# Chunk sums turned back one scan slot later, two copies and the softmax factors at higher priority, factors spread a step later

## The chip, the cores and the metric

The kernel runs on one core of one Trainium2 chip. A core has five engines that run side by side, each through its own queue in order: PE (TensorE, matmuls and transposes, writing to PSUM banks), DVE (VectorE), ACT (ScalarE), POOL (GpSimd) and SP (SyncE, which here issues transfers between main memory and the on-chip buffer). The metric is the time of one execution in microseconds on the device. Three runs of the kernel before gave 5039.27, 5041.66 and 5051.98 us; the median is 5041.66 us.

## What is computed

Two layers on a batch of 8 images of 384 channels and 32x32 positions, that is 1024 tokens, all in 32-bit floats. Layer 0 is a selective scan in both directions over the tokens, plus a gated 3x3 convolution. Layer 1 is causal attention with 6 heads of 64, then a feed-forward part with sign weights and quantised activations (for the first five images alone). Cut to what the change touches:

```python
# layer 0, for u forward and backward; h has 16 states per channel
def step(h, inp):
    dA, dBu, c = inp                      # exp(delta*A), delta*u*B, C
    h = dA * h + dBu
    return h, einsum('bdn,bn->bd', h, c)  # the sum over the 16 states
y = ys + u * D_param
y = y * silu(z)
out = einsum('bld,od->blo', y, out_proj_w)

# layer 1
scores = where(causal, einsum('bhqd,bhkd->bhqk', q, k), -inf)
attn = softmax(scores)
out = einsum('bhqk,bhkd->bhqd', attn, v)
```

## The kernel before

**The scan stream.** For each image (order 0, 1, 2, 3, 5, 6, 4, 7) there are four parts (direction and half of the tokens), 16 states and three chunks of 128 channels. A unit is one chunk, one part and two states: 96 units an image, 768 in all. A unit passes through four stages:

- `s_first` (L585): POOL multiplies delta*u by the row of B into a buffer `g` of 128x1024 (L588). There are six such buffers.
- `s_scan` (L591): for each of the two states ACT makes the decay (L601) into one of two PSUM banks, DVE runs the recurrence in place in `g` (L606), POOL copies the carry (L611) and multiplies `g` by the row of C (L612).
- `s_sum` (L614): PE adds the states up. Eight transposing matmuls against the identity (L620) turn the unit's two 128x512 halves into the one PSUM bank `y`, adding over 4 or 8 successive units of the same chunk and half. With the last of these (`closes`) the bank is emptied into the on-chip buffer: by a copy on ACT (L635) for the first and the last of such a group's runs, by an addition on DVE (L639) for those between. Only then may the next chunk's sums enter the bank.
- `s_gate` (L641): after a chunk's last run, the two partial sums are turned back (L659) onto a matmul of u with diag(D) (L654), in a bank of the kind "pt"; DVE multiplies by the gate (L668), and the result goes to main memory, where the attention of that image reads it. There are 48 such gates.

`slots` (L1093) writes the order down: slot k issues `s_first` of unit k+2, `s_scan` of unit k, `s_sum` of unit k-1 and `s_gate` of unit k-1.

**The other stream.** Beside the slots run the work ahead of the scan for later images and, once an image's scan is through, its attention and feed-forward part. Each is a list of steps with a nominal length; `run` and the loop at the end of the kernel merge the steps with the slots by these lengths. The slots up to number 96 (`first`, L1121) go beside the preparation of the next images, the rest (`others`, L1122) beside attention and feed-forward.

**Attention.** `probabilities` makes, for each pair of heads c and each half g of the queries, the exponentials of the scores in blocks of up to 512 keys, each with its own maximum `nm` and sum `rs`. `weighted_values` (L820) then walks over the 4 or 8 chunks j of keys, one step for each:

- `factors` (L825) at j = 0: from `nm` and `rs` the factor of each block. For g = 0 one reciprocal, for g = 1 six small operations on DVE (L833, L834, L836 to L839) and an exponential on ACT (L835).
- `spread` (L841) at j % 4 = 2: eight small matmuls (L847) spread a block's factors over 64 rows each into a "pt" bank, ACT copies them out (L854).
- `turned` (L856): PE transposes the probabilities (L862) into "pt" banks, ACT copies them (L864).
- `weigh` (L867), one step behind: PE multiplies by the values (L875) into the one bank "av". After a block's fourth chunk DVE multiplies this bank by the spread factors (L889, L891).

PSUM has eight banks: one "y", two "da", two "s", two "pt", one "av".

**What sets the order.** A scheduler puts the instructions into the engines' queues when the kernel is built. It takes, among the instructions that it holds to be ready, the one of the highest priority; priority is the order in which the kernel's text issues them, and `tc.high_priority(offset=60)` counts an instruction as if it had been issued 60 earlier. Waits between engines are put in by the same program. On the chip each queue then runs as it was written.

Of the kernel before, what the change touches and what calls it, by code (L numbers as in the profile page):

```python
# [12 lines left out]
ALU = mybir.AluOpType  # L13
# [23 lines left out]
QT = HB // P  # L37
# [7 lines left out]
AHEAD = 2  # L45
# [9 lines left out]
def kernel(  # L55
# [16 lines left out]
    nc = tc.nc  # L72
# [17 lines left out]
    def mtile(name, n=L):  # L90
        return mid.tile([P, n], F32, name=name, tag="mid")
# [7 lines left out]
    def bank(name, tag=None):  # L99
        if tag is None:  # L100
            turn[0] += 1
            tag = ("s", "pt")[turn[0] % 2]
        return ps.tile([P, HB], F32, name=name, tag=tag, bufs=BANKS[tag])

    def half(h):
        return slice(h * HB, (h + 1) * HB)

    def chunk(c):
        return slice(c * P, (c + 1) * P)
# [434 lines left out]
    class Unit:  # L544
# [6 lines left out]
    units = [  # L551
        Unit(b, part, c, n)
        for b in ORDER
        for part in range(len(PARTS))
        for k in range(NS // SET)
        for c in (range(NC) if k % 2 == 0 else reversed(range(NC)))
        for n in range(k * SET, (k + 1) * SET, 2)
    ]
# [17 lines left out]
    def s_row(u, i):  # L576

        if not u.asks:
            return
        r = sp.tile([P, 2, HB], F32, name=f"bc{i}_{u.name}", tag=f"bc{i}", bufs=4)  # L580
        rows = spilled[u.b, "rows", u.d][i * NS + u.n : i * NS + u.n + 2, half(u.h)]
        load(r, rows.partition_broadcast(P))
        sst["bc", i, u.b, u.part, u.n] = r
# [30 lines left out]
    def s_sum(u):  # L614
        if u.opens:
            sst["y"] = bank(f"y_{u.name}", "y").rearrange("p (j k) -> p j k", k=P)
        y, g = sst["y"], sst.pop(("g", u.name))
        for i in range(2):
            for j in range(QT):
                nc.tensor.matmul(  # L620
                    out=y[:, j, :],
                    lhsT=g[:, i, chunk(j)],
                    rhs=ident,
                    is_transpose=True,
                    start=(u.opens and i == 0 and j == 0),
                    stop=(u.closes and i == 1),
                    skip_group_check=True,
                )
        if not u.closes:
            return  # L630
        key = ("yt", u.b, u.c, u.h)
        if u.run == 0 or u.last:
            tag = {"tag": "yl", "bufs": 1} if u.last else {"tag": "yt", "bufs": 2 * NC}
            yt = sp.tile([P, QT, P], F32, name=f"yt_{u.name}", **tag)
            nc.scalar.copy(yt, y)  # L635
            sst[key] = sst.get(key, []) + [yt]
        else:
            (yt,) = sst[key]
            nc.vector.tensor_tensor(yt, yt, y, ALU.add)  # L639

    def s_gate(u):  # L641

# [31 lines left out]
    def attention(b, emit_ffn, emit):  # L674
# [83 lines left out]
        def at_once(second):  # L758
            return tc.high_priority(offset=HURRY) if second else nullcontext()

        def rows_of(e):
            return slice(e * HD, (e + 1) * HD)
# [57 lines left out]
        def weighted_values(c, g, steps):  # L820


            last = (g + 1) * QT - 1

            def factors():  # L825

                nm, rs = st["nm", c, g], st["rs", c, g]
                st["f", c, g] = mtile(f"f_{b}_{c}_{g}").rearrange("p (k l) -> p k l", k=2)
                if g == 0:
                    nc.vector.reciprocal(rs, rs)  # L830
                    return
                low = small.tile([P, QT, 2, 1], F32, name=f"low_{b}_{c}", tag="low")
                nc.vector.tensor_reduce(low, nm, AX.X, ALU.min)  # L833
                nc.vector.tensor_tensor(nm, low.to_broadcast([P, QT, 2, 2]), nm, ALU.subtract)  # L834
                nc.scalar.activation(nm, nm, AF.Exp)  # L835
                nc.vector.tensor_tensor(rs, rs, nm, ALU.mult)  # L836
                nc.vector.tensor_reduce(low, rs, AX.X, ALU.add)
                nc.vector.reciprocal(low, low)
                nc.vector.tensor_tensor(rs, nm, low.to_broadcast([P, QT, 2, 2]), ALU.mult)  # L839

            def spread(kb):  # L841

                fp = bank(f"f_{b}_{c}_{g}_{kb}", "pt")
                for i in range(QT):
                    for e in range(2):
                        f = st["rs", c, g][:, i, e, kb : kb + 1]
                        nc.tensor.matmul(  # L847
                            out=fp[rows_of(e), chunk(i)],
                            lhsT=f.to_broadcast([P, HD]),
                            rhs=ident,  # L850
                            start=True,
                            stop=True,
                        )
                nc.scalar.copy(st["f", c, g][:, kb, :], fp)  # L854

            def turned(j):  # L856
                cols = slice(max(j - g * QT, 0) * P, HB)
                for e in range(2):
                    pt = bank(f"pt_{b}_{c}_{g}_{j}_{e}", "pt")
                    for i in range(max(j - g * QT, 0), QT):  # L860
                        pr = st["pr", c, g, i, j // QT]
                        nc.tensor.transpose(pt[:, chunk(i)], pr[:, e, chunk(j % QT)], ident)  # L862
                    ptn = ptp.tile([P, HB], F32, name=f"ptn_{b}_{c}_{g}_{j}_{e}", tag=f"ptn{e}")
                    nc.scalar.copy(ptn[:, cols], pt[:, cols])  # L864
                    st["ptn", j, e] = ptn

            def weigh(j):  # L867
                if j % QT == 0:
                    st["av"] = bank(f"av_{b}_{c}_{g}_{j}", "av")
                av = st["av"]  # L870
                cols = slice(max(j - g * QT, 0) * P, HB)
                for e in (1, 0):
                    hd = 2 * c + e
                    with at_once(e == 0):
                        mm = nc.tensor.matmul(  # L875
                            out=av[rows_of(e), cols],
                            lhsT=st["v"][:, j, hd * HD : (hd + 1) * HD],
                            rhs=st["ptn", j, e][:, cols],
                            start=(j % QT == 0),
                            stop=(j % QT == QT - 1),  # L880
                        )
                    if e == 0:
                        pin(mm)
                if j % QT < QT - 1:
                    return
                kb = j // QT
                o, f = st["o"][:, c, half(g)], st["f", c, g][:, kb, :]
                if kb == 0:
                    nc.vector.tensor_tensor(o, av, f, ALU.mult)  # L889
                else:  # L890
                    nc.vector.tensor_tensor(av, av, f, ALU.mult)  # L891
                    nc.vector.tensor_tensor(o, o, av, ALU.add)

            for j in range(last + 1):

                @steps
                def _(j=j):
                    if j == 0:
                        factors()
                    if j % QT == 2:  # L900
                        spread(j // QT)
                    turned(j)
                    if j > 0:
                        weigh(j - 1)

            @steps
            def _():
                weigh(last)
# [184 lines left out]
    def slots(lo, hi):  # L1093
        def at(f, k):
            if 0 <= k < len(units):
                f(units[k])

        def slot(k):
            at(s_load, k + AHEAD + 2)
            at(lambda u: s_row(u, 0), k + AHEAD + 2)  # L1100
            at(lambda u: s_row(u, 1), k + 2)
            at(s_first, k + AHEAD)
            at(s_scan, k)
            at(s_sum, k - 1)
            at(s_gate, k - 1)

        return [(lambda k=k: slot(k), 5.0) for k in range(lo, hi)]

# [9 lines left out]


    per, ahead = len(units) // B, 3  # L1120
    first = slots(-AHEAD - 2, per + 1)  # L1121
    others = slots(per + 1, len(units) + 1)  # L1122

    taps = btile("taps").rearrange("p c l -> p (c l)")[:, : NC * DCONV * P]
    taps = taps.rearrange("p (c k q) -> p c k q", c=NC, k=DCONV)
# [37 lines left out]
    at = 0.0  # L1163
# [57 lines left out]
```

## Time and profile before

| | |
|---|---|
| median of three runs | 5041.66 us |
| the profiled execution's own time | 5052.48 us |
| its span | 5050.7 us |
| instructions | 50731 |
| mean granted TensorE clock | 0.883 |
| L620 sums on PE | 6144, 920.6 us busy |
| L635 copies of the bank on ACT | 96, 580 ns each |
| L639 additions of the bank on DVE | 56, 674 ns each |
| L847 spread of factors on PE | 1152 records, 100.0 us busy |
| L854 copies of spread factors on ACT | 72, 576 ns each |
| L601 decays on ACT | 1536, 691 ns each |
| L606 recurrences on DVE | 1536, 1210 or 1271 ns each |

In the profile's groups the columns are line, engine, operation, result <- operands, shapes and count; then busy time in us and the mean of one in ns; then the idle time of the engine just before these instructions and what ended it. PEld is the loading of weights, which overlaps the matmuls. A line of the wait view names the engine and the line that waited, what it waited for, the total in us, the number of waits and the longest. In the timeline the columns are start and length in us, engine, line, operation; in square brackets the idle time of the engine before it and what ended it.

### The profile page before, as it was taken

How to read it: one execution, taken by the hardware profiler on the slowest of the kernel's cores; microseconds unless marked ns; L12 is line 12 of the kernel's file. 1: busy time of each engine (PE TensorE's matmuls, PEld its weight loads, DVE VectorE, ACT ScalarE, POOL GpSimd, SP SyncE). 2: the span in 40 equal slices, each digit the busy share in tenths (PEclk: the TensorE clock that was granted, in tenths of full speed). 3: DMA queues.
4: the chain of work that ended last, by engine and by line, in shares of the span. 5: the costliest groups of instructions: out<-in, count | busy, mean ns of one | idle time of the engine just before them, and what ended most of it. 6: DMA issues, size and time to landing. Idle time of an engine off the chain costs nothing. (4 is left out here: it accounts for less than half of the span.)

```text
span 5050.7 us, 50731 instructions
## 1 busy us (share of the span) xinstructions
PE 4072.5 (81%) x16458; PEld 2180.7 (43%) x16458; DVE 3605.3 (71%) x4775; ACT 2667.4 (53%) x4850; POOL 3689.9 (73%) x1944
## 2 busy tenths in 40 slices
PE   4687787888888888788788888887787978978899
PEld 1243343444444444344444444443454444444444
DVE  6887988676887767786778867688766666676623
ACT  4565664564554655545656446555465355464426
POOL 0578687896868976778876688867788988888700
PEclk7788797989889889888999889998898989989999
DMA  6554546323453334463334633334533334334210
GB/s 227 204 175 160 200 155 229 109 88 118 152 187 135 119 115 154 139 200 111 103 134 143 213 111 128 110 123 155 194 132 106 118 108 143 109 101 139 88 58 26
DMA packets 365009, 696.35 MB, mean 138 GB/s; under 512 B 30104, under 2 KB 88904, under 8 KB 364744
## 3 DMA queue, kind: packets, MB, share of 16 engines
q1 hardware_dynamic: 355232, 676.97, 40.0%
q10 hardware_dynamic: 9512, 16.15, 0.9%
q8 instruction: 130, 2.13, 0.2%
q14 instruction: 135, 1.11, 0.1%
HBM read 527.33 MB, written 165.68 MB: 137 GB/s over the span
## 5 line engine op out<-in xcount | busy, mean ns | idle before, releaser
L588 POOL TENSOR_TENSOR g<-ud,bc 128x1024 f32<-128x1024 f32 x768 | 1837.9, 2393 | 654.0 <-PE y L620 523.0
L612 POOL TENSOR_TENSOR g<-g,bc 128x1024 f32<-128x1024 f32 x768 | 1819.4, 2369 | 194.9 <-DVE g L606 132.4
L601 ACT ACTIVATE da<-dl,amat 128x512 f32<-128x512 f32 x1536 | 1055.9, 691 | 1515.1 <-DVE g L606 1489.8
L606 DVE TENSOR_TENSOR_SCAN g<-da,g 128x512 f32<-128x512 f32 x768 | 907.7, 1210 | 509.6 <-POOL g L588 496.3
L606 DVE TENSOR_TENSOR_SCAN g<-da,carry,g 128x512 f32<-128x512 f32 x768 | 955.1, 1271 | 403.9 <-POOL g L588 374.5
L620 PE MATMUL y<-ident,g 128*128 128x128 f32 x6144 | 920.6, 297 | 210.3 <-POOL g L612 122.3
L620 PEld LDWEIGHTS y<-ident,g 128*128 128x128 f32 x6144 | 766.9, 153 | 644.3 <-issue 345.5
L786 PE MATMUL s<-k,q 64*128 64x512 f32 (+3 forms) x1152 | 394.6, 602 | 134.6 <-DVE nm L800 113.5
L800 DVE CUSTOM_DVE_ANT_0 pr<-s,cmask 128x512 f32<-128x512 f32 (+3 forms) x576 | 298.9, 544 | 179.3 <-PE s L786 159.9
L810 ACT ACTIVATE pr<-pr,nm 128x512 f32<-128x512 f32 (+3 forms) x576 | 348.4, 606 | 125.1 <-DVE nm L800 123.5
L862 PE MATMUL pt<-ident,pr 128*128 128x128 f32 x1728 | 302.1, 304 | 83.5 <-ACT ptn L864 38.5
L992 PE MATMUL hp<-t,w 128*128 128x512 f32 x720 | 339.3, 618 | 25.4 <-DMA w<-w1s 21.2
L1036 PE MATMUL yp<-h,w 128*128 128x512 f32 x720 | 331.9, 620 | 32.0 <-DMA w<-w2s 27.6
L341 PE MATMUL in<-xn,win 128*128 128x512 f32 x576 | 291.2, 651 | 36.5 <-DVE xc L463 15.9
L862 PEld LDWEIGHTS pt<-ident,pr 128*128 128x128 f32 x1728 | 207.0, 152 | 243.5 <-ACT ptn L864 94.3
L875 PE MATMUL av<-ptn,v 128*64 128x512 f32 (+3 forms) x1152 | 274.3, 559 | 23.2 <-DVE o L889 17.2
L611 POOL COPY carry<-g 128x2 f32<-128x2 f32 x384 | 87.7, 228 | 271.2 <-DVE g L606 271.2
L864 ACT COPY ptn<-pt 128x512 f32<-128x512 f32 (+3 forms) x576 | 254.7, 473 | 55.5 <-PE pt L862 53.5
L725 PE MATMUL qp<-t,wqk 128*128 128x512 f32 x576 | 267.8, 616 | 14.7 <-DVE t L302 12.5
L400 DVE SCALAR_TENSOR_TENSOR loc<-xn,vec,loc 128x496 f32<-128x496 f32 (+3 forms) x384 | 259.5, 722 | 20.3 <-ACT loc L389 19.0
L786 PEld LDWEIGHTS s<-k,q 64*128 64x128 f32 x1152 | 134.8, 206 | 266.5 <-DVE nm L800 190.1
L1036 PEld LDWEIGHTS yp<-h,w 128*128 128x128 f32 x720 | 141.9, 201 | 204.7 <-issue 177.2
(153 smaller groups left out, 4753.4 us busy)
## 6 DMA issues: line engine op xcount, KB each, us to landing
bc<-rows SPq DMA_DIRECT2D x512, 512.0 KB, 4.1
dl<-sdl SPq DMA_DIRECT2D x160, 256.0 KB, 2.9
ud<-sud SPq DMA_DIRECT2D x160, 256.0 KB, 2.7
t<-st SPq DMA_DIRECT2D x63, 512.0 KB, 5.1
su<-u SPq DMA_DIRECT2D x48, 512.0 KB, 3.6
du<-su SPq DMA_DIRECT2D x96, 256.0 KB, 3.8
sdl<-du SPq DMA_DIRECT2D x96, 256.0 KB, 2.9
sud<-du SPq DMA_DIRECT2D x96, 256.0 KB, 2.7
```

What stands on the lines that cost most here:

```text
L341: nc.tensor.matmul(out=mp, lhsT=st["win", c][:, k, i, :], rhs=st["xn"][:, k, half(h)], start=(k == 0), stop=(k == NC - 1),)
L588: pin(nc.gpsimd.tensor_tensor(g, ud, sst["bc", 0, u.b, u.part, u.n], ALU.mult))
L601: nc.scalar.activation(da, sst["dl", u.b, u.c, u.part], AF.Exp, scale=amat[:, u.c, n : n + 1])
L606: nc.vector.tensor_tensor_scan(gi[:, ::step], da[:, ::step], gi[:, ::step], first, ALU.mult, ALU.add)
L612: pin(nc.gpsimd.tensor_tensor(g, g, sst["bc", 1, u.b, u.part, u.n], ALU.mult))
L620: nc.tensor.matmul(out=y[:, j, :], lhsT=g[:, i, chunk(j)], rhs=ident, is_transpose=True, start=(u.opens and i == 0 and j == 0), stop=(u.cl ...
L786: mm = nc.tensor.matmul(out=ss[e][:, : k1 - k0], lhsT=st["q"][rows_of(e), c, chunk(qi)], rhs=st["k"][rows_of(e), c, k0:k1], start=True, st ...
L800: nc.vector.tensor_tensor_reduce(out=x, in0=ss[e][:, :w], in1=mask, scale=-1.0, scalar=-MASKED, op0=ALU.add, op1=ALU.min, accum_out=m,)
L810: nc.scalar.activation(x, x, AF.Exp, bias=m, scale=-1.0, accum_out=rs[:, i, e, kb : kb + 1])
L862: nc.tensor.transpose(pt[:, chunk(i)], pr[:, e, chunk(j % QT)], ident)
L992: nc.tensor.matmul(out=hp, lhsT=st["w1"][:, c, chunk(m % 2)], rhs=st["xn"][:, c, half(h)], start=(c == 0), stop=(c == NC - 1),)
L1036: nc.tensor.matmul(out=yp, lhsT=st["w2", k // 6][:, k % 6, :], rhs=st["h", k // NC][:, k % NC, half(h)], start=(k == 0), stop=(k == NF - 1),)
```

## The change

Four edits, none of which changes what is computed:

- `s_gate` of a unit is issued one slot later, after the sums of the following unit; the slots' range is one longer, and the border between `first` and `others` moves by one.
- The two instructions that empty the bank `y` (L635 and L639) are issued at a priority 60 places higher.
- So are all instructions of `factors`.
- `spread` is issued in the step j % 4 = 3 instead of 2, that is one step after, and in the same step as the block's last `turned`; `weigh` of that last chunk, with the products L889 or L891 that read the factors, follows in the next step as before.

```diff
@@ s_sum
-            nc.scalar.copy(yt, y)
+            with tc.high_priority(offset=60):
+                nc.scalar.copy(yt, y)
             sst[key] = sst.get(key, []) + [yt]
         else:
             (yt,) = sst[key]
-            nc.vector.tensor_tensor(yt, yt, y, ALU.add)
+            with tc.high_priority(offset=60):
+                nc.vector.tensor_tensor(yt, yt, y, ALU.add)
@@ weighted_values
                     if j == 0:
-                        factors()
-                    if j % QT == 2:
+                        with tc.high_priority(offset=60):
+                            factors()
+                    if j % QT == QT - 1:
                         spread(j // QT)
                     turned(j)
                     if j > 0:
@@ slots
             at(s_sum, k - 1)
-            at(s_gate, k - 1)
+            at(s_gate, k - 2)
@@
-    first = slots(-AHEAD - 2, per + 1)
-    others = slots(per + 1, len(units) + 1)
+    first = slots(-AHEAD - 2, per + 2)
+    others = slots(per + 2, len(units) + 2)
```

## The prediction

> **What bounds the kernel now.** I read the page first (shares, then the costliest groups), then the waits, then three lines of code by their instructions, then the timeline around single stalls.
>
> ```profile
> PE 4072.5 (81%) x16458; PEld 2180.7 (43%) x16458; DVE 3605.3 (71%) x4775; ACT 2667.4 (53%) x4850; POOL 3689.9 (73%) x1944
> ...
> L588 POOL TENSOR_TENSOR g<-ud,bc 128x1024 f32<-128x1024 f32 x768 | 1837.9, 2393 | 654.0 <-PE y L620 523.0
> L612 POOL TENSOR_TENSOR g<-g,bc 128x1024 f32<-128x1024 f32 x768 | 1819.4, 2369 | 194.9 <-DVE g L606 132.4
> ```
>
> No engine is full. POOL does nothing but the scan: 768 units of two products, 2.39 + 2.37 us each, 3657 us in all, from 129 to 4812 us. So the scan stage lasts as long as POOL's work plus its idle time, and the largest piece of that idle time is 523 us in 203 waits for PE's sums (L620): a product of unit k+6 needs one of six buffers `g`, and PE frees it by turning unit k. PE works through one queue in order, so whatever stalls it there delays the sums behind it. The chain of waits holds only the last 450 us (from 4599 us) and says nothing of the stage itself.
>
> Which PE stalls the diff touches, from the wait view:
>
> ```profile
> PE yb L659 <- ACT yt L635: 58.7, 22, 9.8
> PE f L847 <- DVE rs L839: 57.3, 15, 8.5
> ...
> PE y L620 <- DVE yt L639: 44.0, 16, 7.2
> ...
> PE pt L862 <- ACT f L854: 34.3, 26, 3.9
> ```
>
> Each has total us, times, longest. The instructions of L847 add a second reason for the same place, a queue entry of ACT behind the factors, and those of L620 the other half of the bank waits:
>
> ```profile
>   DVE rs L839: 57.3, 15
>   ACT da L601: 16.2, 3
> ```
>
> ```profile
>   DVE yt L639: 44.0, 16
>   ACT yt L635: 29.4, 10
> ```
>
> So 73.5 us of PE stand still before the spread of the factors, 58.7 us before the turn-back of a chunk, 73.4 us before the next chunk's sums. Do these reach POOL? One stall in PE's timeline, and POOL's first product after it:
>
> ```profile
> 4080.99 1.08 PE L875 MATMUL av<-ptn,v 128*64 128x512 f32 x4
> 4087.83 1.98 PE L847 MATMUL f<-ident,rs 128*64 128x128 f32 x16 [5.75 <-DVE rs L839]
> ...
> 4093.08 1.04 PE L620 MATMUL y<-ident,g 128*128 128x128 f32 x8
> ```
>
> ```profile
> 4094.20 2.36 POOL L588 TENSOR_TENSOR g<-ud,bc 128x1024 f32<-128x1024 f32 x1 [6.55 <-PE y L620]
> ```
>
> PE waits 5.75 us for the factors; the sum behind them comes at 4093.08, and POOL has then been idle 6.55 us. I looked at all 17 stalls of over 1 us before L847: each is followed within 3 to 9 us by such a POOL wait, together 88 us. For the 22 turn-back stalls I took for each the smaller of the stall and POOL's waits for PE from 2 us before to 12 us after it: 42 of 58.7 us reach POOL. For the bank waits before L620 the same count gives only 18 of 73.4 us.
>
> **What the Trainium skill says.** "SBUF — State Buffer", Who interferes with whom: a VectorE instruction with two SBUF inputs and a GpSimd one that reads SBUF exclude each other, the later one blocks fully. The trace agrees: the factor steps L834, L836, L839 on 16 columns take 0.15 to 0.18 us at their shortest, but 1.3, 1.4 and 0.8 us in the mean and once 8.92 us, while POOL multiplies. So factors are late for a reason that no priority removes; only a later reader does. "TensorE: Matmul & The Clock Gate", Architectural detail: PE's queue only pulls weight loads ahead, ScalarE and VectorE are strictly first in, first out. The trace agrees: while PE stood from 4082 to 4087.8 us no other matmul ran. "ScalarE: Activation LUTs", What ACT_TABLE_LOAD costs: about 1283 ns a load; the trace shows 1283.
>
> **The change part by part.** Durations are of the profiled execution: span 5050.7 us, 5052.5 us with what lies around it; the median of the runs, 5041.66, is 10.8 lower. What a step is moved past I counted in the two built programs' queues, which hold no times.
>
> *Spread a step later.* The 1152 matmul records of L847 and the 72 copies L854 stay. Against the scan's units all attention work moves by about 0.9 unit, the f matmuls by 1.75, so they come 0.85 unit later than before among their neighbours. A unit lasts (4812 - 129)/768 = 6.1 us, so 5.2 us more cover; I use 5. Taking 5 from each of the 18 stalls leaves 7 us (3.5 of it from the 8.5 us one). Gone: 66 us. Nearly all of it reached POOL, but PE then runs on into readers of the same late DVE and ACT queues; that share is not to be read from the trace, between none and all of it. I take 70% kept: -47 us (bounds -66 and 0).
>
> Its price: the reader of the factors, L889/L891 on DVE, now starts a median 9.2 us after the copy L854 ends, at least 2.2 us. With the copy 5 to 6 us later, 6 to 10 of 72 readers would wait, 10 to 18 us of DVE with scans behind them: +5 us (bounds 0 and 18). In blocks on the diagonal the f bank is followed by one turn instead of two before its bank is wanted again (L862 <- f, 34.3 us today): +5 (0 to 10).
>
> *Gate a slot later.* Same instructions: 48 diagonal matmuls, 384 turns, 48 products L668, their loads and stores on SP, all one slot on. Before, the first to wait for the copied chunk is mostly the turn-back; after, always the next chunk's first sum, because the bank `y` is single. So this wait is moved, not removed. In 47 such places the PE work queued ahead of the first waiter has a median of 1.7 us before and 3.4 after, at 0.14 us for a turn and 1.12 for a 512-wide matmul; in the trace the 1.7 take 1.13 us, so 3.4 take 2.3, 1.2 us more cover. Taking 1.2 from each of the 22 stalls leaves 35: 24 us gone, 42/58.7 of it reaching POOL: -17 us (bounds -42 and 0). SP prefetches `us` and `z` when their single buffers come free; a slot's delay of both load and use cancels. The run of slots is one longer and all other work starts one slot later against the scan: in the tail the transpose of L960, which opens the last feed-forward product, stands behind one more unit of sums, 4.7 us of POOL: +5 us (0 to 6).
>
> *Copies and factors at higher priority.* No duration changes. In ACT's queue the copies stand a mean 4.7 units behind the scan's newest decay before and 4.8 after, in DVE's 8.0 and 7.9; factors move with their neighbours (0.83 unit against 0.9). The delay of a copy (start a mean 2.3 us after the sums on ACT, 2.9 on DVE) comes from scans and decays ahead of it that wait for POOL. -3 us (bounds -20 and 0).
>
> *Side effects.* Everything is reordered a little: four more table loads on ACT, 4 x 1.283 us = 5.1 us, beside an engine that is 53% busy, +1; three or four copies go from DVE to ACT, nothing.
>
> Sum: -47 +5 +5 -17 +5 -3 +1 = -51 us, so 5001.5 in the profile's time, a ratio of 0.990; on the median, 4991 us.
>
> **The rivals.**
>
> *The stall only moves on* (19%). PE gets past the factors, but the next thing in its queue needs DVE or ACT, and those were late. For: in the 8.92 us case DVE itself was held, and PE stands 109 us before scores L786 for DVE. Against: in the example it was followed by transposes, weights and sums that were ready. Then perhaps 20 of the 66 us and 5 of the turn-backs' 17 stay gained; with the costs of 16 us (5 + 5 + 5 + 1) that is -9 us, 5033 us.
>
> *Everything lands* (14%). All 66 us, 42 us of turn-backs, and copies prompt enough to give the 18 us of bank waits: -126 + 16 = -110, 4932 us.
>
> *The factors' reader holds DVE* (17%; slower). Where L889 waits for L854 in DVE's strict queue, scans wait behind it, then POOL. Cover between spread and reader falls from 8.9 to 5.0 us of PE work by the same counting. It needs ACT to be late: the copy starts a mean 1.03 us after the f matmuls, at most 5.3. At 1.5 us for each of 72 readers this costs 108 us against gains of 56 (the sum without the reader's 5): +52, 5094 us. It decides from 56/72 = 0.8 us a reader. Against: today's slack is 5.3 us or more for nine readers in ten.
>
> **How the numbers follow.** The forecast has 50%, its own range 4955 to 5026. All over, 4945 leaves out the better part of the large gain, 5060 takes in the stall that moves on and the light form of the slower rival; the bounds of the parts, all added on one side, would be -128 and +39 us, 4914 and 5081 on the median. This kernel's measurement can tell 0.3%, 15 us, from no change: faster than 5026.5 is the forecast, the large gain and nearly half of the moving stall (72%), the rest of the latter is within (11%), the reader's wait is slower (17%).
>
> **What would show it.** Right: waits of L847 for L839 and L601 fall from 73.5 to about 10 us; those of L659 for L635 go to nothing, those of L620 for L635 and L639 rise from 73 to about 105 us; POOL's waits for L620 fall from 523 to about 460. The slower rival would show L889 or L891 waiting for L854, absent today. The forecast is wrong if POOL's idle for L620 falls and its idle for L606 (132 before L612, 271 before L611) rises by as much, or if L847's waits stay.

## The result, and the profile after

The changed kernel takes 4982.55 us (median of four runs, 4979.25 to 4992.14) against 5040.47 us of the kernel before in the same comparison: a ratio of 0.9884, 95% interval 0.9863 to 0.9905. The forecast was 4991 us. The span of its profiled execution is 4982.3 us against 5050.7, 68 us less.

The page of the changed kernel, the engines' shares and POOL's two groups. Lines of the code have moved by two or three from L637 on: what was L639 is L641, L659 is L661, L847 is L849, L864 is L866, and the copy L635 is L636.

```profile
PE 4058.8 (81%) x16458; PEld 2192.3 (44%) x16458; DVE 3607.8 (72%) x4771; ACT 2668.1 (54%) x4858; POOL 3696.0 (74%) x1944
...
L588 POOL TENSOR_TENSOR g<-ud,bc 128x1024 f32<-128x1024 f32 x768 | 1840.4, 2396 | 579.8 <-PE y L620 452.0
L612 POOL TENSOR_TENSOR g<-g,bc 128x1024 f32<-128x1024 f32 x768 | 1822.1, 2373 | 251.7 <-DVE g L606 157.8
```

Work is the same to within 14 us on every engine; only the waiting has changed. POOL's idle time for PE's sums fell from 523 to 452 us; its idle time for the scans before L612 rose from 132 to 158, that before the carries L611 fell from 271 to 206. Over all of POOL's instructions, 71 us of waiting for PE and 47 us for DVE went, 12 us of other gaps went, and 48 us of waiting for transfers came: 1090 us of idle time before, 1008 after.

Three more lines of the wait view of before (total us, times, longest):

```profile
POOL carry L611 <- DVE g L606: 271.2, 28, 49.0
...
PE pt L862 <- ACT ptn L864: 38.5, 37, 2.7
...
PE av L875 <- ACT ptn L864: 6.0, 9, 1.6
```

and the wait view of the changed kernel:

```profile
POOL g L588 <- PE y L620: 452.0, 202, 14.1
POOL carry L611 <- DVE g L606: 205.8, 26, 46.7
...
PE y L620 <- ACT yt L636: 77.0, 22, 11.9
...
PE y L620 <- DVE yt L641: 56.2, 17, 7.5
...
PE pt L864 <- ACT ptn L866: 55.1, 43, 3.8
...
PE av L877 <- ACT ptn L866: 33.9, 16, 4.0
...
POOL g L612 <- DMA bc<-rows: 30.1, 6, 13.1
...
POOL g L612 <- DMA gy<-sgy: 15.9, 1, 15.9
```

PE's idle time before the spread, by the instructions of L849 on PE:

```profile
  ACT ptn L866: 14.3, 11
  DVE rs L841: 3.9, 4
  ACT da L601: 1.2, 1
```

So the stalls before the spread are gone (57.3 + 16.2 us to 3.9 + 1.2), and the turn-back L661 no longer waits for the copied chunk at all (58.7 us to none). But two waits have grown: the next chunk's sums wait 77.0 + 56.2 = 133.2 us for the emptied bank instead of 73.4, which is within about 1 us what both places cost together before (132.1); and PE now waits for the copies of the turned probabilities before transposes, weights and spread, 55 + 34 + 14 = 103 us, where it was 38.5 + 6.0 = 44.5. With the wait for the f bank (34.3 us before, 15.8 after) the spread's places save some 28 us of PE's time, and the gate's none, while 58 us went from the measured time. So PE's own waits do not add up to the gain, and the experiments have to tell where it comes from.

### The profile page after: what moved, and what is told of

Read it like the earlier page. It is cut to its first block, busy times and chain, and to the rows that moved or that the text cites. A ratio compares the mean times of both kernels' runs of the same rounds, so it can differ in the third digit from the quotient of the medians.

```text
span 4982.3 us, 50788 instructions
## 1 busy us (share of the span) xinstructions
PE 4058.8 (81%) x16458; PEld 2192.3 (44%) x16458; DVE 3607.8 (72%) x4771; ACT 2668.1 (54%) x4858; POOL 3696.0 (74%) x1944
## 5 line engine op out<-in xcount | busy, mean ns | idle before, releaser
L588 POOL TENSOR_TENSOR g<-ud,bc 128x1024 f32<-128x1024 f32 x768 | 1840.4, 2396 | 579.8 <-PE y L620 452.0
L612 POOL TENSOR_TENSOR g<-g,bc 128x1024 f32<-128x1024 f32 x768 | 1822.1, 2373 | 251.7 <-DVE g L606 157.8
L601 ACT ACTIVATE da<-dl,amat 128x512 f32<-128x512 f32 x1536 | 1057.3, 691 | 1532.5 <-DVE g L606 1498.3
L606 DVE TENSOR_TENSOR_SCAN g<-da,g 128x512 f32<-128x512 f32 x768 | 906.5, 1210 | 475.4 <-POOL g L588 457.2
L606 DVE TENSOR_TENSOR_SCAN g<-da,carry,g 128x512 f32<-128x512 f32 x768 | 953.3, 1271 | 384.2 <-POOL g L588 354.1
L620 PE MATMUL y<-ident,g 128*128 128x128 f32 x6144 | 949.1, 303 | 266.7 <-POOL g L612 123.1
L620 PEld LDWEIGHTS y<-ident,g 128*128 128x128 f32 x6144 | 789.3, 156 | 714.4 <-issue 418.9
L788 PE MATMUL s<-k,q 64*128 64x512 f32 (+3 forms) x1152 | 384.5, 600 | 128.9 <-DVE nm L802 110.5
L864 PE MATMUL pt<-ident,pr 128*128 128x128 f32 x1728 | 304.0, 309 | 93.6 <-ACT ptn L866 55.1
L864 PEld LDWEIGHTS pt<-ident,pr 128*128 128x128 f32 x1728 | 217.7, 155 | 245.0 <-ACT ptn L866 110.3
L866 ACT COPY ptn<-pt 128x512 f32<-128x512 f32 (+3 forms) x576 | 255.3, 472 | 49.8 <-PE pt L864 48.4
L400 DVE SCALAR_TENSOR_TENSOR loc<-xn,vec,loc 128x496 f32<-128x496 f32 (+3 forms) x384 | 259.9, 721 | 19.5 <-ACT loc L389 18.2
L611 POOL COPY carry<-g 128x2 f32<-128x2 f32 x384 | 87.0, 226 | 205.9 <-DVE g L606 205.8
```

The lines of the kernel that those rows point to most:

```text
L588: pin(nc.gpsimd.tensor_tensor(g, ud, sst["bc", 0, u.b, u.part, u.n], ALU.mult))
L601: nc.scalar.activation(da, sst["dl", u.b, u.c, u.part], AF.Exp, scale=amat[:, u.c, n : n + 1])
L606: nc.vector.tensor_tensor_scan(gi[:, ::step], da[:, ::step], gi[:, ::step], first, ALU.mult, ALU.add)
L612: pin(nc.gpsimd.tensor_tensor(g, g, sst["bc", 1, u.b, u.part, u.n], ALU.mult))
L620: nc.tensor.matmul(out=y[:, j, :], lhsT=g[:, i, chunk(j)], rhs=ident, is_transpose=True, start=(u.opens and i == 0 and j == 0), stop=(u.cl ...
L788: mm = nc.tensor.matmul(out=ss[e][:, : k1 - k0], lhsT=st["q"][rows_of(e), c, chunk(qi)], rhs=st["k"][rows_of(e), c, k0:k1], start=True, st ...
```

## The experiments

Each kernel was run 4 to 19 times against the kernel before on the same chip; ratios are to that kernel, with their 95% interval. The traces named are one execution of each. The theory to test (A): the later spread carries the gain and the other parts only move a wait. Rival B: gate and copies carry a third or more. Rival C: any new order of the queues moves this kernel by half a per cent.

**One part alone.** First the later spread:

```diff
-                    if j % QT == 2:
+                    if j % QT == QT - 1:
```

> The kernel before with the spread of the factors one step later and nothing else. Theory A (PE's stalls before the spread reach POOL, the rest of the change only moves a wait): ratio 0.987 to 0.992, nearly the whole of the change's 0.9884; waits of L847 for L839 and L601 fall from 73.5 us to under 15, POOL's waits for L620 from 523 to about 450. Rival B (the later gate and the prompter copies carry a third or more of the gain): ratio 0.993 to 0.997. Rival C (any new order of the queues moves this kernel by half a per cent either way): anything from 0.98 to 1.0, with POOL's idle time for L620 not following PE's stalls before L847.

Measured: 5021.29 us against 5042.08, ratio 0.9962 (0.9947 to 0.9977): 0.4%, a third of the change and less than A expected, in the range of B. The stalls went as foreseen, and came back one place further. The instructions of L862, the transposes, in the kernel with the later spread:

```profile
L862 PE MATMUL pt<-ident,pr x1728: 272/273/477, 942.6 to 5001.2; 128*128 128x128 f32 x192
its engine sat idle before it (us, times) until:
  ACT ptn L864: 81.1, 44
  DVE zh L668: 17.9, 9
  ACT f L854: 16.0, 19
```

and of L875, the weights, in the same kernel:

```profile
its engine sat idle before it (us, times) until:
  ACT ptn L864: 46.6, 27
  DVE o L889: 18.0, 10
who waited for it (us, times):
  DVE o L889: 44.7, 15
```

Before the spread it waits 0.8 us for L839 and 1.2 for L601, so 71.5 us went. Before transposes, weights and spread it waits 81.1 + 46.6 + 17.7 = 145.4 us for L864 where it waited 44.5: 101 us came. The wait for the f bank before the transposes fell from 34.3 to 16.0. PE's idle time in all fell by 9 us, POOL's wait for PE by 22, the span by 32.

Then the later gate, together with the border that moves with it:

```diff
-            at(s_gate, k - 1)
+            at(s_gate, k - 2)
...
-    first = slots(-AHEAD - 2, per + 1)
-    others = slots(per + 1, len(units) + 1)
+    first = slots(-AHEAD - 2, per + 2)
+    others = slots(per + 2, len(units) + 2)
```

> The kernel before with the gate one slot later (and the slots' range one longer) and nothing else. Theory A: the wait for the copied chunk moves from the turn-back L659 (58.7 us to 0) to the next chunk's sums L620 (73.4 us to about 130), sum unchanged; ratio 0.998 to 1.002. Rival B: the sum falls by 20 us or more and the ratio is 0.993 to 0.997. Rival C: a ratio off by 0.4% or more with the sum unchanged.

Measured: 5021.39 us, ratio 0.9955 (0.9942 to 0.9967): as much as the spread, B's number. The turn-back no longer waits. The sums L620 in this kernel:

```profile
  POOL g L612: 140.9, 56
  ACT yt L635: 52.2, 19
  DVE yt L639: 47.3, 16
```

52.2 + 47.3 = 99.5 us where both places held 132.1, so 33 us less here, which is B's sign too. Whether these 33 us are what gives the time is asked below.

Then the copies' priority:

```diff
-            nc.scalar.copy(yt, y)
+            with tc.high_priority(offset=60): nc.scalar.copy(yt, y)
...
-            nc.vector.tensor_tensor(yt, yt, y, ALU.add)
+            with tc.high_priority(offset=60): nc.vector.tensor_tensor(yt, yt, y, ALU.add)
```

> The kernel before with the two instructions that empty the bank y at the higher priority and nothing else. Theory A: the sum of PE's waits for L635 and L639 stays within 20 us of 132 us, since what the copies wait for is ahead of them in the queue for other reasons; ratio 0.997 to 1.002. Rival B: the waits fall by 40 us or more, ratio under 0.996. Rival C: a ratio off by 0.4% or more with the waits unchanged.

Measured: 5048.12 us, ratio 1.0009 (0.9999 to 1.0019). The bank's waits are 34.7 + 38.6 us before the sums and 54.7 before the turn-back, 128 in all against 132. The priority does nothing that can be measured when alone, as A expected. In the trace's order of ACT it moved 34 of the 96 copies forward, but not past the scan's decays: they stand 4.6 units behind the newest decay in the mean, with it and without.

**The change without its spread.** Here the edit is to the changed kernel:

```diff
-                    if j % QT == QT - 1:
+                    if j % QT == 2:
```

> The changed kernel with the spread put back to the step j % 4 = 2: later gate, prompter copies and factors stay. Theory A: the stalls before L847 come back (50 to 80 us) and with them the time, ratio to the kernel before 0.997 to 1.002. Rival B: 0.990 to 0.996. A third reading, that the higher priority of the factors does the work of the later spread, would show as under 30 us of stalls before L847 and a ratio near 0.99.

Measured: 5031.75 us, ratio 0.9979 (0.9972 to 0.9987); PE waits before the spread 63 us again (41.3 for L839, 15.7 for L601, 6.2 for the copies of turned probabilities). A expected this, and the factors' priority does not do the later spread's work. Against this kernel the complete change is 49 us faster (5031.75 to 4982.55), while alone the same edit gave 21 us: the parts are not a sum. And this kernel is slower than the later gate alone (5021.39, intervals apart), so in this company the two priorities cost about 10 us.

**Is it the gate, or what moves with it?** The later gate needs a longer range of slots, and with the border between `first` and `others` all other work starts one slot later against the scan. This kernel takes that alone:

```diff
-    first = slots(-AHEAD - 2, per + 1)
-    others = slots(per + 1, len(units) + 1)
+    first = slots(-AHEAD - 2, per + 2)
+    others = slots(per + 2, len(units) + 2)
```

> The kernel before with the slots' range one longer and the border between the first slots and the others one later, the gate staying in its slot: all other work starts one slot later against the scan, as in the change, but no gate moves. If the gate's own move gives the gain of the later-gate kernel (0.9955): ratio 0.999 to 1.002 and PE's waits before L659 near 59 us as before. If the shift of the other work against the scan gives it: ratio 0.994 to 0.997 with those waits still there.

Measured: 5009.72 us against 5044.52, ratio 0.9932 (0.9919 to 0.9944), at least as good as with the gate moved (the intervals just touch). The turn-back L659 in this kernel still waits as before:

```profile
its engine sat idle before it (us, times) until:
  ACT yt L635: 56.1, 25
```

So the border's shift alone is enough for the gain of the later gate; a gate moved without the border was not run. Where the gain comes, the traces tell by the time at which POOL starts the first product of a unit, here minus that of the kernel before in us (one profiled execution each; the last row is the end of the span):

```text
unit   before   spread   gate  border  border+2  spread+gate  +factors  the change
  96    768.4    -2.3   -11.5    -8.1      2.8       -6.4        -9.4      -11.3
 192   1354.9   -10.1   -21.7   -23.2    -23.8      -29.3       -32.8      -32.5
 320   2161.6    -3.9   -45.0   -43.9    -37.9      -46.1       -49.6      -48.6
 480   3119.1   -10.7   -33.9   -30.7    -20.1      -51.2       -51.5      -43.5
 576   3727.7   -18.8   -38.1   -37.4    -30.3      -61.2       -58.8      -48.7
 672   4248.7   -20.3   -35.9   -35.7    -41.5      -76.0       -76.2      -59.3
 end   5050.7   -32.1   -30.4   -47.5    -36.4      -76.1       -83.2      -68.4
```

Gate and border run together to unit 672. Both win some 45 us in the first 320 units and, swings of some ten us in the table aside, nothing after; these units lie in the stretch in which the scan shares DVE with the preparation of later images (its last convolution, L400, is at unit 531 of the kernel before). Had the copied chunk's wait been what counts, the gate would have to gain all along: the 48 gates lie six to an image. In the last stretch the gate gives back what the border keeps.

What is won early is mostly a wait of POOL for DVE. In the first 320 units POOL waits for the recurrences (before L611 and L612) 278 us in the kernel before, 240 with the later gate and 219 with the border; for PE's sums it waits 185, 179 and 177 us. Two stretches of POOL's timeline at the same place of the work, first of the kernel before:

```profile
1231.08 2.36 POOL L588 TENSOR_TENSOR g<-ud,bc 128x1024 f32<-128x1024 f32 x1
1260.27 2.36 POOL L612 TENSOR_TENSOR g<-g,bc 128x1024 f32<-128x1024 f32 x1 [26.83 <-DVE g L606]
```

then of the kernel with the border moved:

```profile
1228.77 2.35 POOL L588 TENSOR_TENSOR g<-ud,bc 128x1024 f32<-128x1024 f32 x1
1249.75 2.35 POOL L612 TENSOR_TENSOR g<-g,bc 128x1024 f32<-128x1024 f32 x1 [18.62 <-DVE g L606]
```

and what DVE did meanwhile in the kernel before:

```profile
1234.79 3.97 DVE L400 SCALAR_TENSOR_TENSOR loc<-xn,vec,loc 128x496 f32<-128x496 f32 x6
1249.48 1.22 DVE L1002 TENSOR_REDUCE mxh<-h 128x1 f32<-128x1024 f32 x1 [10.72 <-ACT h L1000]
...
1257.68 2.45 DVE L606 TENSOR_TENSOR_SCAN g<-da,carry,g 128x512 f32<-128x512 f32 x2
```

DVE worked off the convolutions, then stood 10.72 us at the head of its queue for an activation of the feed-forward part, with the scan behind it. One slot's shift changes what stands ahead of the scan in such places; in this one 8 us of POOL's time are saved.

**More of the same shift.** The border two and four slots later (`per + 3`, `per + 5` and the ends to match).

> The kernel before with all other work two slots later against the scan instead of one (gate in its place, no other edit). If the scan's lead over the other work is what gives the gain of one slot (0.9932): at least as much again or the same, 0.986 to 0.994. If one slot happened to fall well (where long work on DVE meets the scan's stages): anything between 0.992 and 1.004, not in line with one slot.

> The same with four slots. If the lead gives the gain: 0.982 to 0.994, less the price of the tail, about 5 us a slot. If it is a matter of how the two streams happen to meet: between 0.992 and 1.006, and no order among one, two and four slots.

Measured: 5017.37 and 5027.63 us against 5045.7, ratios 0.9944 (0.9929 to 0.9959) and 0.9959 (0.9944 to 0.9974). One, two, four slots: -35, -28, -18 us. The first slot gives the gain; by the medians each further one costs 5 to 7 us, though the intervals of neighbours overlap. The ratio of two slots lies just above the range expected of the lead, and in that of two streams that happen to meet well; the ratio of four fits both, if the price of the tail is counted. So the ratios do not decide. The traces speak against one common mechanism, for the three gains are made of different waits. Against the kernel before, POOL waits with one slot 30 us less for PE and 38 less for DVE; with two, 14 us more for PE and 65 less for DVE; with four, 93 us less for PE and 15 more for DVE (one trace each; that of four slots is of the slowest of its seven runs). That all three gain is shown, and for one slot that the early part went from waits on DVE; why a lead gains is not.

**The spread one step earlier.**

```diff
-                    if j % QT == 2:
+                    if j % QT == 1:
```

> The kernel before with the spread one step earlier (j % 4 = 1) and nothing else. If the time follows the cover between factors and spread: PE's waits before L847 grow from 73.5 us to 150 us or more, POOL's waits for L620 with them, ratio 1.006 to 1.02. If a stall that is taken from L847 comes back elsewhere in the queue, so that the place matters little: waits before L847 grow, those for L864 before the transposes and weights fall, and the ratio is 0.998 to 1.004.

Measured: 5043.37 us against 5044.52, ratio 1.0000 (0.9990 to 1.0009). The waits of the kernel with the earlier spread:

```profile
PE f L847 <- DVE rs L839: 70.8, 18, 6.4
...
PE pt L862 <- ACT ptn L864: 17.0, 22, 1.8
```

They hardly grew before the spread (73.5 to 77 us with the other reasons) and fell before the transposes (for L864 from 38.5, for the f bank from 34.3 to 1.2), while those of the weights for L864 rose from 6.0 to 14.3. In the trace's order of PE the f matmuls moved ahead by only half a unit against the sums, where the later spread moved them 0.9 unit back, and the transposes moved a third of a unit back. So the edit took away little of the cover. The ratio is that of the second reading, but the growth that both readings expected before L847 did not come, and this run does not decide between them. PE's idle time in all is 953 us here and 961 with the later spread, though the latter is 22 us faster: PE's idle sum does not rank these kernels.

**Together, and without what does not pay.** Later spread and later gate; then the same with the factors' priority:

> Later spread and later gate together, no priorities. If the two gains (0.9962 and 0.9955 alone) simply add: 0.9917, and the priorities owe the rest of the change's 0.9884. If the two parts help each other: 0.9870 to 0.9895 without any priority. If the priorities cost, as the drop from 0.9955 to 0.9979 between the later gate alone and the same with both priorities suggests: below 0.9870.

> Later spread, later gate and the factors' higher priority; the copies keep theirs. Against the same without the factors' priority it tells what that priority gives: if the factors' priority is what completes the change, 0.987 to 0.989 here and 0.991 to 0.993 without it; if neither priority matters, the two are within 0.15% of each other.

Measured: 4981.01 us, ratio 0.9880 (0.9865 to 0.9896), and 4968.91 us, ratio 0.9854 (0.9840 to 0.9867), both against 5044.52. The two parts alone would give 0.9917; together they give more, the whole of the change, with no priority. In the traces POOL's wait for PE's sums falls from 523 to 501 us with the spread alone, to 499 with the gate alone, and to 441 with both.

One rival was not separated. The granted clock, the mean share of its full speed that TensorE got, was 0.879 to 0.882 in the five runs with the later gate alone, 0.884 to 0.889 with both, and 0.881 to 0.888 in the kernel before. For the same 16458 matmuls PE was busy 4086 us with the gate alone, 4044 with both and 4072 before. So part of the difference between apart and together may be the clock and not the queues.

The factors' priority may add 0.2%: the intervals just touch, and by the table most of the difference lies before any attention and at the end, so it is not shown to come from the factors.

The complete change differs from the second only by the copies' priority, and its ratio is 0.3% higher (the intervals just touch). With the loss of 10 us above, this says that in this company the copies' priority probably costs. The table has the loss build up from unit 320 to 672. Of the second kernel:

```profile
POOL g L588 <- PE y L620: 452.2, 196, 14.1
...
PE y L620 <- ACT yt L635: 49.6, 17, 8.6
...
PE y L620 <- DVE yt L639: 45.9, 16, 7.0
```

PE waits for the bank 49.6 + 45.9 = 95.5 us without the copies' priority and 133.2 with it. The copies are not later for it: from the last sum to the end of the copy it is 3.2 us in the mean without it and 3.0 with it. But PE has less other work queued before the next chunk's first sum, 4.8 us in the median instead of 5.5, so it stands there sooner.

This wait does not explain the loss, though, for POOL waits for PE's sums just as long, 452.2 and 452.0 us. What POOL has more is waits for transfers, 171 us against 128, two of them alone of 15.9 us at unit 421 and 13.1 at unit 436; 20 us less of waiting for DVE make up for part of it. The kernel without the spread, which also has the copies' priority, has waits for transfers of 15.9 and 13.3 us at the same two units, and the kernels with the later gate but not this priority have none of over 1 us there. The loss thus goes with late transfers; how the priority makes them late was not followed. The granted clock differs too, 0.8845 in the mean of the change's runs and 0.8878 without the copies' priority.

With the border instead of the gate (later spread, factors' priority, border one slot later):

> The kernel before with the parts that gained, and without those that did not: later spread, factors at the higher priority, all other work one slot later against the scan; the gate stays in its slot and the copies keep their priority. If the gate's own move is a cost (0.9932 without it against 0.9955 with it): 0.981 to 0.985, faster than the change and than later spread, later gate and factors (0.9854). If the later spread needs the gate's move to pay: 0.986 to 0.990.

Measured: 4974.61 us against 5045.7, ratio 0.9862 (0.9844 to 0.9879). By the median better than the change, but not told apart from 0.9884 nor from 0.9854. Border and spread alone would give 0.9894, so the extra gain is there without the gate: its own move is not needed, and not shown to cost.

**The new stall's copies at higher priority.** Onto the version with 0.9854:

```diff
-                    nc.scalar.copy(ptn[:, cols], pt[:, cols])
+                    with tc.high_priority(offset=60): nc.scalar.copy(ptn[:, cols], pt[:, cols])
```

> Later spread, later gate and the factors' priority (0.9854), and the copies of the turned probabilities (the line after the transposes L862) at the same higher priority. With the spread later, PE's stalls moved to these copies: about 57 us before the transposes, 34 before the weights, 14 before the spread. If the copies' place in ACT's queue is the cause: those waits fall by a third or more and the ratio is 0.980 to 0.984. If ACT is late for what stands ahead of it anyway, as with the copies of the chunk sums: waits within 15 us, ratio 0.984 to 0.988.

Measured: 4982.02 us against 5043.8, ratio 0.9882 (0.9865 to 0.9898). PE's waits for these copies went from 56.8 + 34.2 + 13.9 to 74.6 + 33.5 + 13.4 us. The priority moved 204 of the 576 copies forward in the trace's order of ACT, by less than one instruction in the mean over all. So it hardly moves them, and what it does move gains nothing; the medians say that it costs 13 us. Whether a truly earlier place would help was not tested.

The best median measured is that of later spread, later gate and factors' priority, without that of the copies: 4968.91 us. Rival C in its plain form, that any new order moves this kernel by half a per cent, is out: the copies' priority alone and the earlier spread reordered the queues and gave 1.0009 and 1.0000.

## Why the forecast came true, point by point

- *What bounds the kernel.* Held: no engine is full, work is unchanged, and the gain is idle time of POOL (1090 us before, 1008 after, over all reasons). POOL's waits for L606, whose rise would have been the sign of a wrong forecast, fell by 40 us (271.2 + 132.4 to 205.8 + 157.8). The forecast had no such gain on DVE, nor the 48 us more of waits for transfers.
- *Spread a step later, -47 + 5 + 5.* The stalls vanished as worked out (73.5 to 5 us against 7 foreseen). The share kept, taken as 70%, is not a number of its own: alone the edit gave 21 us, beside the later gate 40 (5021.39 to 4981.01, two comparisons), beside the change's other parts 49 (5031.75 to 4982.55, likewise). Alone, the rival "the stall only moves on" was right, and it named the mechanism, though not the place: the copies of the turned probabilities. Of the two prices, the f bank's went the other way (34.3 to 16 us), and no wait of L889 for L854 came up; DVE waits for PE there instead, 32 us in the change where it was 15 before. The extra cover was sized right, the share that reaches the end was not known.
- *Gate a slot later, -17 + 5.* The size is of the order of the 21 us of the edit alone, but by luck: the mechanism was wrong. The wait moved as said, from L659 to L620. The gain comes with the other work's shift against the scan, which the forecast had only as a cost of the tail; that shift alone is worth 35 us.
- *Copies, -3.* Alone no change; beside the rest a cost of 14 us by the medians (4968.91 to 4982.55, two comparisons). That no priority makes them prompt agrees with the waits staying at 128 us in the kernel with the copies' priority alone, and with their unchanged place behind the decays. (For the additions on DVE the traces have 4.3 units behind the newest scan before and 4.2 after, where the forecast counted 8.0 and 7.9.) That the scans and decays ahead of them make them late is argued, not tested. Factors: 12 us by the medians, not clear of noise.
- *The sum*, -51 us against -58 measured, is right within the range, in part by luck. Spread and gate with their prices were put at -37 and -12 us; alone they gave -21 and -21, together -64, and that surplus of the pair was not foreseen. The priorities, put at -3, gave +2 in all (4981.01 to 4982.55, two comparisons). Of what was to show it, L847's and L659's waits and POOL's 460 us were met (452); L620's waits for the bank were 133 rather than 105; without the copies' priority they are 95 to 99, so the extra cover worked and the priority took it away again, without POOL waiting longer for it.
- *The slower rival* did not come: no reader of the factors holds DVE.

Open: why spread and gate gain more together than apart, and what share of that is the granted clock; why a shift of one, two or four slots gains about alike; and how the copies' priority leads to late transfers.

## What to carry to other kernels

Before crediting a moved instruction with a gain, run the move's side effects alone: here the shift of a loop's border that came with the later gate gave the whole of its gain. A stall removed from an in-order queue can come back at the next instruction that waits for the same late engines; what reaches the end depends on what else is changed, so test an edit both alone and by taking it out of the whole. Before a grown wait is blamed for a loss, look whether the engine that sets the pace waits longer for it: here PE's wait grew by 38 us and POOL's wait for PE not at all. And a higher priority need not make an instruction early: none of the trials of it here (copies alone, copies and factors in company, turned probabilities) showed a gain clear of noise.

## What the runs showed of the hardware

The small factor steps on DVE with two operands in the on-chip buffer (72 of them, 16 columns, 0.15 us at the shortest) mostly take no longer than one product of POOL: in every run the third longest is 2.3 us or less, a product 2.36. But in the kernel before and in three others (later gate; later spread and gate; border two slots later) a single one took 8.9 us, in the kernel before from 4499.39 to 4508.31 us while POOL ran four products end to end. In the kernels with the later spread alone, without the spread, and with border, spread and factors one took 7.1, 5.7 and 3.6 us, and in that with the border moved two took 3.0. Each of these nine ended 0.03 to 0.04 us after the end of a POOL product, of the second, third or fourth that it had run beside. So a step that has lost to POOL once can lose again to POOL's next instruction when that follows at once, and the scans behind it on DVE are held with it. It happened at most twice in 72; the changed kernel has no such step above 2.3 us.
